# Tanh of the cell state beside the sums in PSUM, a rule for GpSimd's long operations, more buffers for the image's chunks, and new constants for the planner

## The chip, the cores and the metric

The kernel runs on one core of a Trainium2 chip. A core has five engines that run side by side and meet through semaphores: TensorE (PE in the profile, with PEld for its weight loads), VectorE (DVE), ScalarE (ACT), GpSimd (POOL) and SyncE (SP), which here issues all transfers. The metric is the device time of one execution in microseconds; lower is better. Everything is computed in fp32.

## The reference

The input x has 8 images of 56 x 56 positions with 256 channels. Two layers follow each other, cut here to what matters:

```python
# layer 0
x = x + attn0(_gn(x))     # group norm over each image; regional attention: an image is 7 x 7
                          # regions of 8 x 8; each takes the 4 best regions by mean query and key,
                          # and each query the best 32 of these 256 keys (top_k, softmax);
                          # plus a 3 x 3 depthwise convolution of v, then a projection
# layer 1, on the 3136 tokens of each image
t = t + attn1(_ln_t(t))   # attention over 7 neighbouring tokens
t = t + ffn(_ln_t(t))     # a recurrence over the 3136 tokens, for 8 images at once:
def step(carry, xs):
    h, c = carry
    xi_t, xf_t, xg_t, xo_t = xs
    i_t = jax.nn.sigmoid(xi_t + h @ V_i)
    g_t = jnp.tanh(xg_t + h @ V_c)
    o_t = jax.nn.sigmoid(xo_t + h @ V_o)
    c_new = h * c + i_t * g_t
    h_new = o_t * jnp.tanh(c_new)
    return ((h_new, c_new), h_new)
```

## The kernel before

The work comes in two kinds that share all engines. The **attention work** is cut into 56 units: 7 rows of regions (448 tokens each) times 8 images. A unit computes queries and values (`queries_and_lepe`), goes through 7 regions (`region`), projects (`project`), attends over neighbours and makes the recurrence's input terms (`window_attention`). In a region, VectorE does most: four rounds of MAX8 and MATCH_REPLACE8 on 128 x 256 scores for each of four groups of heads find the 32 best keys; GpSimd subtracts what is left from the exponentials (`pe`, 128 x 256). Before an image's first unit, `norm_and_route` reads the image twice in 7 chunks of 448 tokens: `stats(p)` takes sums of a chunk, `keys_values(p)` normalizes a chunk on VectorE, multiplies it by the weights on TensorE, copies keys (`ks`) and values (`vs`) out on ScalarE, and stores them to `kd` and `vd`, from where regions gather them (`kg`, `vg`). A chunk is the tile `xchunk`, with 2 buffers, as have `ks` and `vs`.

The **recurrence** is one chain of 3136 steps (`recurrence`). A step has six instructions that wait for each other: 16 matmuls in one bundle add h times V to a bank of PSUM in which the input terms already stand (`sums`, two banks, two steps to a bank; the terms come by DMA into `r_gin` and are copied in by ScalarE, `place_terms`); VectorE transposes the bank (`r_tr`); ScalarE takes tanh of it into the tile `r_cell`; VectorE's scan makes the new cell state (`r_c`, two inputs, both in SBUF); ScalarE takes its tanh (`r_tc`, in SBUF); VectorE's scalar_tensor_tensor makes h (`r_hs`, from `r_cell` and `r_tc`, both in SBUF). Beside that chain ScalarE makes `r_half`, and GpSimd multiplies it by h into `r_cell` for the next step: this small product is "GpSimd's part of a step". Steps of the first rows run among the attention work of the next row, since a step needs the tokens of all 8 images; the last 451 steps (`step_apart`) run when no other work is left, with the matmuls, the transpose and the first tanh split in two.

The order of all instructions is made when the kernel is built, by a planner written in the kernel (class `_Plan`). Every instruction is recorded with an estimate (`_time`) of how long it holds its engine (`held`) and when its result is there (`late`). `run` then walks through time: whenever an engine is free, it takes the ready instruction of the best rank. Steps of the chain have rank 0, attention work rank 1. An instruction that is not of the chain is taken only if it would end before the next instruction of the chain is expected on that engine, plus `SLACK`; for GpSimd the next "pair" counts, an instruction of VectorE with more than one tensor input (`op.pair`). `at` counts the chain's instructions that have been placed, six to a step. Where TensorE would idle longer than `FILL`, a matmul into a spare bank is put in. The result is one fixed order for each engine's queue; on the chip each queue runs in that order, and instructions wait there only for their data.

Of the kernel before, what the change touches and what calls it, by code (L numbers as in the profile page):

```python
# [10 lines left out]
F32 = mybir.dt.float32  # L11
# [6 lines left out]
SP = mybir.EngineType.SP  # L18

P = 128  # L20
C = 256
NWIN = 7
R = 8
W = NWIN * R
S = R * R
NREG = NWIN * NWIN
ROW = NWIN * S
# [5 lines left out]
QB = 112  # L33
# [11 lines left out]
UJ = C // J  # L45
GJ = GATES * UJ
# [11 lines left out]
HOP = 70  # L58
FAR = 10**12
FILL = 250  # L60
SLACK = {"PE": 120, "DVE": 120, "ACT": 60, "POOL": 60, "SP": 1000}


def _shape_of(shape, pattern, sizes):
# [37 lines left out]
def _time(engine, name, view, reads, args, kw):  # L102

    n = max([_count(v) for v in [view] + reads])
    if engine == "SP":
        return 650, 2600 + n // 2
    if engine == "PE":
        held = 160 if name == "transpose" else 5 * _count(view) // 3 + 110
        return held, held + 200
    if engine == "POOL":  # L110
        t = 180 + 15 * n // 7
        return (1050, 1050) if ALU.pow in args else (t + 90, t)
    if engine == "ACT":
        t = 5 * n // 7 + 100
        if kw.get("accum_out") is not None:
            return t + 150, t + 260
        if isinstance(kw.get("bias"), _View) or view.buf.banks:
            return t + 120, t + 200
        return t + 20, t + 110
    held = 25 * n // 24 + 60  # L120
    if name == "reciprocal":
        return 20 * n // 3 + 60, 20 * n // 3 + 150
    if name == "transpose":
        return held + 40, held + 120
    if name == "tensor_tensor_scan":
        return 2 * n + 80, 2 * n + 170
    if name == "match_replace":
        return held + 65, held + 150
    if name == "scalar_tensor_tensor":
        return held + 20, held + 100  # L130
    return held, held + 90
# [97 lines left out]
class _Plan:  # L229
# [71 lines left out]
    def add(self, engine, traces, reads, writes, held, late):  # L301
        op = _Op()
        op.engine, op.trace, op.held, op.late = engine, traces, held, late
        op.rank, op.chain = self.mode
        op.rank = (op.rank, len(self.ops))
        op.before, op.takes, op.start = {}, [], None
        op.pair = engine == "DVE" and len(reads) > 1
        self.ops.append(op)
        for views, write in ((reads, False), (writes, True)):
            for v in views:  # L310
                self._depend(op, v, write)
                if v.buf.pool is not None:
                    if not v.buf.users:
                        op.takes.append(v.buf)
                    if not v.buf.users or v.buf.users[-1] is not op:
                        v.buf.users.append(op)
# [25 lines left out]
    def run(self, tc, fill):  # L342
# [24 lines left out]
        at, made, events = 0, {}, []  # L367
# [24 lines left out]
                    return t  # L392
            return FAR

        filled = 0
        while len(done) < len(ops) + filled:
            moved = False
            for e in engines:
                if free[e] > now:
                    continue  # L400
                while later[e] and later[e][0][0] <= now:
                    _, rank, op = heappop(later[e])
                    insort(ready[e], (rank, op))
                if not ready[e]:
                    continue
                until = expected(e) + SLACK[e]
                for i, (rank, op) in enumerate(ready[e]):
                    if not op.chain and now + op.held > until:
                        continue
                    if any(b.free and not self._room(b, made, now) for b in op.takes):  # L410
                        continue
                    del ready[e][i]
                    op.start = now
                    free[e] = now + op.held
                    heappush(events, free[e])
                    heappush(events, now + op.late + HOP)
                    done.append(op)
                    for b in op.takes:
                        if b.free:
                            made.setdefault(id(b.tag), []).append(b)  # L420
                    for b, gap in op.before.items():
                        b.due = max(b.due, now + gap)
                        b.open -= 1
                        if not b.open:
                            opened(b)
                    if op.chain:
                        at += 1
                    moved = True
                    break
            if not moved and free["PE"] <= now:  # L430

                due = min([expected("PE")] + [op[0] for op in later["PE"][:1]])
                if FILL < due - now < FAR // 2:
                    op = _Op()
                    op.trace, op.start = [fill], now
                    filled += 1
                    done.append(op)
                    free["PE"] = now + FILL
                    heappush(events, free["PE"])
                    moved = True  # L440
            if not moved:
                while events and events[0] <= now:
                    heappop(events)
                if not events:
                    raise RuntimeError("the plan has stopped")
                now = heappop(events)
# [30 lines left out]
def _layers(ctx: ExitStack, tc, a, out):  # L477
# [9 lines left out]
    nc = tc.nc  # L487
    nb = x.shape[0]
# [7 lines left out]
    two = ctx.enter_context(tc.tile_pool(name="two", bufs=2))  # L496
    small = ctx.enter_context(tc.tile_pool(name="small", bufs=6))
    image = ctx.enter_context(tc.tile_pool(name="image", bufs=1))
    rwork = ctx.enter_context(tc.tile_pool(name="r_work", bufs=3))
# [3 lines left out]
    ps_r = ctx.enter_context(tc.tile_pool(name="ps_r", bufs=1, space=PSUM))  # L503
# [60 lines left out]
    for dy in range(3):  # L564
        rows = slice(dy * HD, (dy + 1) * HD)
        for n in range(24):
            k, dx, g = n // 12, n // 4 % 3, n % 4
# [13 lines left out]
    for t in cells:  # L581

        nc.vector.memset(t, 0.0)
        for at in (0, CELL + 2):
            e = t[:, at : at + CELL].rearrange("p (n e) -> p n e", e=3)
# [2 lines left out]
    gins = [const.tile([P, XB, GJ], F32, name=f"r_gin{i}") for i in range(2)]  # L588
    for t in gins:
        nc.gpsimd.memset(t, 0.0)  # L590
    sums = [ps_r.tile([P, 2 * GJ], F32, name=f"r_sum{i}") for i in range(2)]
    for t in sums:
        nc.tensor.matmul(
            t, gins[0].rearrange("p t g -> p (t g)")[:, :P], wu[:, 0, : t.shape[1]],
            start=True, stop=True, skip_group_check=True,
        )
# [12 lines left out]
    raw, nc = nc, _Plan(nc)  # L609
# [6 lines left out]

    cells = [nc.fixed(t, (P, 3 * CELL + 4)) for t in cells]
    gins = [nc.fixed(t, (P, XB, GJ)) for t in gins]
    sums = [nc.fixed(t, (P, 2 * GJ), banks=1) for t in sums]
    state = {"h": h0}  # L620
    t2, xg = [], []

# [9 lines left out]
    def norm_and_route(b, im):  # L632
# [1 line left out]


        def chunk(p):
            xc = two.tile([P, 2, ROW], F32, name="xchunk")
            nc.sync.dma_start(
                xc, xt[b, :, p * ROW : (p + 1) * ROW].rearrange("(k q) s -> q k s", k=2)
            )  # L640
            return xc
# [67 lines left out]
        def keys_values(p):  # L709
            xn = chunk(p)  # L710
            normalize(im, xn)
            ks = two.tile([P, NWIN, 2, S], F32, name="ks")
            for m in range(2):
                pk = bank()
                for k in range(2):
                    nc.tensor.matmul(
                        pk[:, :ROW], w0[:, k, C + m * P : C + (m + 1) * P],
                        xn[:, k, :], start=(k == 0), stop=(k == 1),
                    )
                nc.scalar.activation(  # L720
                    ks[:, :, m, :], pk[:, :ROW].rearrange("p (q s) -> p q s", s=S),
                    AF.Identity, bias=b0[:, 2 + m : 3 + m],
                )
            nc.sync.dma_start(
                im["kd"][p * NWIN : (p + 1) * NWIN].rearrange("q p s -> p q s"),
                ks.rearrange("p q k s -> p q (k s)"),
            )
            for i in range(NQB):
                pv = bank()
                for k in range(2):  # L730
                    nc.tensor.matmul(
                        pv[:QB, :C], xn[:, k, i * QB : (i + 1) * QB], w0[:, k, 2 * C :],
                        start=(k == 0), stop=(k == 1),
                    )
                vs = two.tile([QB, C], F32, name="vs")
                nc.scalar.copy(vs, pv[:QB, :C])
                t0 = p * ROW + i * QB
                nc.sync.dma_start(im["vd"][t0 : t0 + QB], vs)
# [504 lines left out]
    def place_apart(t, part):  # L1243
        cols = slice(0, 2 * UJ) if part == "ci" else slice(2 * UJ, 3 * UJ)
        nc.scalar.copy(apart(t, part), gins[t // XB % 2][:, t % XB : t % XB + 2, cols])

    def compact(t):
        return t.rearrange("p (c x) -> p c x", x=32)[:, :, :nb]

    def recurrence(blk):  # L1250
# [14 lines left out]
        def step(t):  # L1265
# [7 lines left out]
            with nc.rank(0, chain=True):  # L1273
# [17 lines left out]
                    c.rearrange("p k b e -> p (k b e)"), cell[:, :CELL],  # L1291
                    cell[:, CELL + 2 : 2 * CELL + 2], 0.0, ALU.mult, ALU.add,
                )
                tch = rwork.tile([P, 2, nb], F32, name="r_tc")
                nc.scalar.activation(tch, c[:, :, :, 2], AF.Tanh, scale=0.5)
                hn = hs[:, :, t, :]
                nc.vector.scalar_tensor_tensor(
# [214 lines left out]
```

## Time and profile before

The three runs before took 9910.28, 9912.33 and 9922.73 us (median 9912.33). The profiled execution took 9902.77 us, with a span of 9901.1 us from the first to the last instruction. Its first step of the recurrence ends near 1500 us; the first split step begins at 8890 us.

| stretch of the span, us | length | PE busy | DVE busy | ACT busy | POOL busy |
|---|---|---|---|---|---|
| 0 to 1500: attention of the first row, norms of all images | 1500 | 1239 | 1053 | 678 | 396 |
| 1500 to 9000: attention and steps together | 7500 | 6987 | 6610 | 4801 | 2707 |
| 9000 to 9901: the chain alone | 901 | 778 | 386 | 385 | 91 |

How to read it: busy time is the sum of an engine's instructions in that stretch. Weight loads are counted apart. PE's time holds the spare matmuls too (2208 us in the whole span). In the page's groups a row gives the engine, the operation, the tiles written and read, shape, count, busy time and mean duration, and behind the second bar the engine's idle time before these instructions and what ended it. Line L290 is the planner's one place of recording, so tiles tell the instructions apart.

### The profile page before, as it was taken

What the parts mean: (1) busy time and instruction counts of PE and PEld (TensorE: products, weight loads), DVE (VectorE), ACT (ScalarE), POOL (GpSimd) and SP (SyncE); (2) the same over time, 40 slices, a digit from 0 to 9 for tenths busy, and PEclk for the clock granted to TensorE, in tenths of its full rate; (3) what the DMA queues carried; (4) which work ended last, traced back from release to release, by engine and by line L of the source; (5) the groups of instructions that cost most, each with busy time, mean ns of one, the idle gap of its engine ahead of it and who ended that gap; (6) DMA issues with size and microseconds to landing.
All of it is one profiled execution on the core that took longest, in us unless ns stands there. A gap on an engine that the chain in (4) does not pass through costs nothing.

```text
span 9901.1 us, 320002 instructions
## 1 busy us (share of the span) xinstructions
PE 9004.2 (91%) x111782; PEld 5270.8 (53%) x111782; DVE 8048.2 (81%) x32969; ACT 5863.0 (59%) x22855; POOL 3193.8 (32%) x7550
## 2 busy tenths in 40 slices
PE   6888889999999999999999999999999999998888
PEld 4445445555555555555545555555555545557777
DVE  5686688999998999989989899898988888874444
ACT  3444456666666666666666666666666666654444
POOL 1222233333333333333333333333333333331111
PEclk9989889999999999999999999999999999999999
DMA  5544423233233232332323323233232222220000
GB/s 156 150 131 132 121 82 86 75 80 82 76 82 81 71 83 77 81 81 71 84 74 81 81 72 86 74 81 79 74 85 76 72 73 79 75 53 21 21 21 19
DMA packets 838243, 786.81 MB, mean 79 GB/s; under 512 B 94734, under 2 KB 794244, under 8 KB 836628
## 3 DMA queue, kind: packets, MB, share of 16 engines
q1 hardware_dynamic: 836628, 766.33, 29.1%
q8 instruction: 884, 14.48, 0.6%
q14 instruction: 731, 5.99, 0.2%
HBM read 527.08 MB, written 238.88 MB: 77 GB/s over the span
## 4 chain that ended last, share of the span: by engine, by line
DVE 46%; PE 16%; ACT 12%; DMA 5%; issue 5%; SPq 1%; POOL 1%; DVEq 0%; ACTq 0%; POOLq 0%
DVE left L290 13%; DVE top L290 10%; PE r_sum L290 9%; DVE r_c L290 7%; DVE r_tr L290 7%; ACT r_cell L290 5%; PE mm L290 5%; DVE r_hs L290 4%; DMA vshift<-lines 2%; ACT r_tc L290 2%; DMA lines<-v 2%; PE pt_av L290 1%; DVE st L290 1%; PE spare L604 1%; ACT et L290 1%
## 5 line engine op out<-in xcount | busy, mean ns | idle before, releaser
L290 PE MATMUL r_sum<-r_v,r_hs 128*8 128x192 f32 (+1 forms) x57376 | 2650.4, 307 | 496.1 <-DVE r_hs L290 439.1
L290 POOL TENSOR_TENSOR r_cell<-r_hs,r_half 128x16 f32<-128x16 f32 x3136 | 722.6, 230 | 4643.2 <-DVE r_hs L290 2588.8
L604 PE MATMUL spare<-ident 128*32 128x128 f32 x15904 | 2208.1, 277 | 1.5 <-POOL ident masks.py:199 1.5
L290 ACT ACTIVATE r_cell<-r_tr 128x48 f32<-128x48 f32 (+2 forms) x3587 | 911.7, 259 | 2156.4 <-DVE r_tr L290 2069.5
L290 PEld LDWEIGHTS r_sum<-r_v,r_hs 128*8 128x8 f32 x57376 | 1233.5, 89 | 1739.1 <-DVE r_hs L290 1397.5
L290 DVE MATCH_REPLACE8 left<-top,left 128x256 f32<-128x256 f32 x4704 | 1899.5, 407 | 0.2 <-issue 0.2
L604 PEld LDWEIGHTS spare<-ident 128*32 128x32 f32 x15904 | 1596.3, 110 | 471.9 <-issue 373.2
L290 DVE MAX8 top<-left 128x8 f32<-128x256 f32 x4704 | 1841.1, 406 | 1.4
L290 DVE STREAM_TRANSPOSE r_tr<-r_sum 128x192 f32<-128x192 f32 (+2 forms) x3587 | 1231.9, 350 | 631.1 <-PE r_sum L290 607.0
L290 DVE TENSOR_TENSOR_SCAN r_c<-r_cell 128x48 f32<-128x48 f32 x3136 | 945.5, 302 | 542.3 <-ACT r_cell L290 382.3
L290 POOL TENSOR_TENSOR pe<-pe,left 128x256 f32<-128x256 f32 x1568 | 1142.1, 733 | 731.2 <-ACT left L290 590.7
L290 ACT ACTIVATE r_tc<-r_c 128x16 f32<-128x16 f32 x3136 | 701.1, 224 | 508.9 <-DVE r_c L290 469.9
L290 ACT COPY r_sum<-r_gin 128x384 f32<-128x384 f32 (+2 forms) x1795 | 807.7, 450 | 14.1 <-DMA r_gin<-xgd 7.8
L290 ACT ACTIVATE pe<-sc,nmax 128x256 f32<-128x256 f32 x1568 | 684.9, 472 | 173.0 <-DVE left L290 103.4
L290 PE MATMUL pt_av<-ident,pe 128*128 128x128 f32 x3136 | 690.5, 297 | 91.2 <-POOL pe L290 67.2
L290 ACT ACTIVATE left<-left,nmax 128x256 f32<-128x256 f32 x1568 | 749.1, 500 | 35.5 <-DVE left L290 26.3
L290 DVE SCALAR_TENSOR_TENSOR r_hs<-r_cell,r_tc 128x16 f32<-128x16 f32 x3136 | 587.9, 187 | 188.8 <-ACT r_tc L290 183.7
L290 PE MATMUL mm<-wu,xlT 128*112 128x512 f32 (+2 forms) x1856 | 728.1, 509 | 3.2 <-ACT gs L290 2.5
L290 ACT ACTIVATE et<-top,nmax 128x32 f32<-128x32 f32 x1568 | 497.3, 318 | 332.8 <-DVE top L290 325.4
L290 DVE MAX8 top<-sc 128x8 f32<-128x256 f32 x1568 | 618.2, 412 | 78.6 <-PE sc L290 75.2
L290 ACT COPY pts<-pt_av 128x256 f32<-128x256 f32 x1568 | 566.0, 361 | 169.5 <-PE pt_av L290 166.8
L290 ACT ACTIVATE r_half<-r_c 128x16 f32<-128x16 f32 x3136 | 651.4, 208 | 0.0
(128 smaller groups left out, 11793.0 us busy)
## 6 DMA issues: line engine op xcount, KB each, us to landing
kg<-kd SPq DMA_DIRECT2D x1568, 64.0 KB
vg<-vd SPq DMA_DIRECT2D x1568, 64.0 KB
vshift<-lines SPq DMA_DIRECT2D x336, 232.0 KB
xgd<-gs SPq DMA_DIRECT2D x224, 336.0 KB
r_gin<-xgd SPq DMA_DIRECT2D x1568, 48.0 KB
xchunk<-xt SPq DMA_DIRECT2D x112, 448.0 KB
lines<-v SPq DMA_DIRECT2D x112, 290.0 KB
xn<-xh SPq DMA_DIRECT2D x56, 560.0 KB
```

Of the source, the lines that this page charges most:

```text
L290: method(*[v.real() if isinstance(v, _View) else v for v in args], **{k: v.real() if isinstance(v, _View) else v for k, v in kw.items()},)
L604: raw.tensor.matmul(spare[:32, :P], ident[:, :32], ident, start=True, stop=True, skip_group_check=True)
```

## The change

In the step, the tanh of the cell state is written to 16 more columns of the PSUM bank that holds the step's sums, and the instruction that makes h reads it there:

```diff
-    sums = [ps_r.tile([P, 2 * GJ], F32, name=f"r_sum{i}") for i in range(2)]
+    sums = [ps_r.tile([P, 2 * GJ + 2 * nb], F32, name=f"r_sum{i}") for i in range(2)]
...
+    def cell_tanh(t):
+
+        bank = sums[t // 2 % 2]
+        return bank[:, 2 * GJ :].rearrange("p (k b) -> p k b", k=2)
...
-                tch = rwork.tile([P, 2, nb], F32, name="r_tc")
+                tch = cell_tanh(at)
                 nc.scalar.activation(tch, c[:, :, :, 2], AF.Tanh, scale=0.5)
```

This is in `step` alone; `step_apart` is not edited and keeps its tile `r_tc`. In the planner, instructions of GpSimd that hold it for more than 400 ns get a condition, a "pair" is now one with two inputs in SBUF, and some constants change:

```diff
-SLACK = {"PE": 120, "DVE": 120, "ACT": 60, "POOL": 60, "SP": 1000}
+LONG = 400
+SLACK = {"PE": 60, "DVE": 120, "ACT": 60, "POOL": 60, "SP": 1000}
...
     if engine == "SP":
-        return 650, 2600 + n // 2
+        return 650, 2400 + 9 * n // 4
...
-        if isinstance(kw.get("bias"), _View) or view.buf.banks:
+        if isinstance(kw.get("bias"), _View) or view.buf.banks and n > UJ:
...
-        op.pair = engine == "DVE" and len(reads) > 1
+        op.pair = engine == "DVE" and sum(not v.buf.banks for v in reads) > 1
...
-        filled = 0
+        filled = tied = 0
...
+                    if e == "POOL" and op.held > LONG and (at % 6 > 3 or tied < at // 6):
+
+                        continue
...
                     if op.chain:
                         at += 1
+                    elif e == "POOL" and op.rank[0] == 0:
+                        tied += 1
```

The chunk's tile `xchunk` gets 4 buffers instead of 2, `ks` 3, `vs` 4. No computation is added or removed; both programs have 26691 instructions of VectorE and 21057 of ScalarE.

More of the change, by code (lines that the diff above doesn't have):

```diff
@@ L590, in _layers @@
         nc.gpsimd.memset(t, 0.0)
-    sums = [ps_r.tile([P, 2 * GJ], F32, name=f"r_sum{i}") for i in range(2)]
+    sums = [ps_r.tile([P, 2 * GJ + 2 * nb], F32, name=f"r_sum{i}") for i in range(2)]
     for t in sums:
+        t = t[:, : 2 * GJ]
         nc.tensor.matmul(
@@ L618, in _layers @@
     gins = [nc.fixed(t, (P, XB, GJ)) for t in gins]
-    sums = [nc.fixed(t, (P, 2 * GJ), banks=1) for t in sums]
+    sums = [nc.fixed(t, (P, 2 * GJ + 2 * nb), banks=1) for t in sums]
     state = {"h": h0}
@@ L636, in chunk @@
         def chunk(p):
-            xc = two.tile([P, 2, ROW], F32, name="xchunk")
+            xc = two.tile([P, 2, ROW], F32, name="xchunk", bufs=4)
             nc.sync.dma_start(
@@ L711, in keys_values @@
             normalize(im, xn)
-            ks = two.tile([P, NWIN, 2, S], F32, name="ks")
+            ks = two.tile([P, NWIN, 2, S], F32, name="ks", bufs=3)
             for m in range(2):
@@ L734, in keys_values @@
                     )
-                vs = two.tile([QB, C], F32, name="vs")
+                vs = two.tile([QB, C], F32, name="vs", bufs=4)
                 nc.scalar.copy(vs, pv[:QB, :C])
```

## The prediction

> **What bounds the kernel now.** I read the slices of the page first, then the timeline of some steps in the middle, the groups by form, the waits of the first 1500 us, and the timeline of one stretch there.
>
> ```profile
> span 9901.1 us, 320002 instructions
> DVE  5686688999998999989989899898988888874444
> ACT  3444456666666666666666666666666666654444
> ```
>
> VectorE is busy for about 90% from slice 7 to slice 36, less before (norms) and after (the chain alone). From the first step (1500.2 us) to the first split step (8890.1) lie 2685 steps, 2.75 us each. Averaged over them, the chain's path is: end of r_hs to the transpose 1088 ns, transpose 373, to the gates' tanh 101, that tanh 268, to the scan 105, scan 309, to the cell's tanh 36, that tanh 224, to r_hs 55, r_hs 190. The shortest times that recur for these pieces add up to about 2512 ns, so some 236 ns a step are lost to other work. Two causes stand in the timeline:
>
> ```profile
> 5003.66 0.73 POOL L290 TENSOR_TENSOR pe<-pe,left 128x256 f32<-128x256 f32 x1 [1.24 <-ACT left L290]
> 5003.85 0.64 DVE L290 TENSOR_TENSOR_SCAN r_c<-r_cell 128x48 f32<-128x48 f32 x1 [0.15 <-ACT r_cell L290]
> ...
> 5009.49 0.26 DVE L290 TENSOR_TENSOR_SCAN r_c<-r_cell 128x48 f32<-128x48 f32 x1
> 5009.78 0.22 ACT L290 ACTIVATE r_tc<-r_c 128x16 f32<-128x16 f32 x1
> ...
> 5011.24 0.37 DVE L290 STREAM_TRANSPOSE r_tr<-r_sum 128x192 f32<-128x192 f32 x1
> 5011.71 0.27 ACT L290 ACTIVATE r_cell<-r_tr 128x48 f32<-128x48 f32 x1 [1.59 <-DVE r_tr L290]
> ```
>
> A scan that meets a long GpSimd operation takes 0.64 us, one that doesn't 0.26. And the cell's tanh starts 0.03 us behind the scan, the gates' tanh 0.10 behind the transpose: in the program the first waits for one semaphore, the second for two. Over the trace these gaps are 34 and 94 ns (the same tile with one wait: 34), so a second wait costs 60 ns where the late one comes first.
>
> **The change, part by part.** Every term is set against the span of 9901.1.
>
> ```profile
> L290 DVE TENSOR_TENSOR_SCAN r_c<-r_cell 128x48 f32<-128x48 f32 x3136 | 945.5, 302 | 542.3 <-ACT r_cell L290 382.3 <-POOL gs L290 20.8 <-POOL pe L290 5.4
> L290 DVE SCALAR_TENSOR_TENSOR r_hs<-r_cell,r_tc 128x16 f32<-128x16 f32 x3136 | 587.9, 187 | 188.8 <-ACT r_tc L290 183.7
> L290 DVE SCALAR_TENSOR_TENSOR r_res<-mm,r_res 128x128 f32<-128x128 f32 x392 | 102.8, 270 | 2.1 <-PE mm L290 1.6 <-issue 0.5
> L290 DVE SCALAR_TENSOR_TENSOR s<-mm,mask 112x118 f32<-112x118 f32 x224 | 58.8, 263 | 15.2 <-PE mm L290 15.1
> L290 ACT COPY r_sum<-r_gin 128x256 f32<-128x256 f32 x226 | 82.1, 363 | 1.8 <-DMA r_gin<-xgd 1.8
> L290 ACT COPY r_sum<-r_gin 128x128 f32<-128x128 f32 x226 | 61.8, 274 | 0.8 <-DMA xgd<-gs 0.3 <-ACT r_cell L290 0.3
> ```
>
> *r_hs meets GpSimd no more: -52.* Its median is 174 ns; 191 of 3136 are longer by more than 20, together 52 us, nearly all under a long GpSimd operation (median there 443). Forms with one input in PSUM, r_res and s, have the same median under a long GpSimd operation (270, 262) as without (267, 261). With r_tc in PSUM, r_hs becomes such a form. Bounds -52 and 0.
>
> *The scan still meets it: +16.* The scan keeps two inputs in SBUF. 536 scans are lengthened, by 138 us in all; by the programs' order 508 of them (132 us) by a long operation that stands on GpSimd's queue just ahead of GpSimd's part of the coming step: its data are there early, so it starts about 1.3 us before the h that the planner put it behind. The new condition should forbid that place, but `tied` counts every rank-0 instruction of GpSimd, also the memset of `r_hs` in the first block, and so runs one ahead. In the order of the changed program 1299 long operations still stand there, against 1167; none is left between scan and r_hs (35 before). 138 x 1299/1167 = 154. Bounds -138 (collisions gone) and +60 (every added one hits).
>
> *The cell's tanh: +20.* Of the 2685 steps, 1605 get a second wait: the tanh now writes a bank that TensorE writes, so the sequencer waits for VectorE (late) and the instruction for TensorE (long done). Behind it on ScalarE stands r_half, which feeds GpSimd's part; that part ends a median 1.47 us before the next scan, so only r_hs is late. The write itself: copies into PSUM take 274 ns at 128 elements, 363 at 256, 495 at 384; the lines through them give 159 to 196 at 16, against 208 for r_half's copy into SBUF: 12 to 49 less, I take 30. From scan to r_hs VectorE has other work too. Where it is nothing or one short instruction (56% of the steps) the wait ends at 290 ns by the tanh; with one MATCH_REPLACE8 (28%) VectorE itself ends at 295; with two (15%) later. So a step with the second wait loses 0.56 x 30 + 0.28 x 25 = 24 ns, one without gains 0.56 x 30 = 17: 1605 x 24 - 1080 x 17 = +20 us. With no gain from PSUM +79, with 49 about -15. The split steps keep r_tc and don't change.
>
> *r_hs reads PSUM: -14.* r_res, s and part (277 at 128), carried to 16 elements at 1.04 ns an element, give 153 to 160 against 174: 17 less, which reaches the chain where TensorE and not VectorE ends the wait for the transpose, about 30% of the steps: 17 x 0.3 x 2685. The dearest such row, t (476 at 256, with a pointer scalar too), gives 226: +52 a step, 140 us if all of it counts. Most rows lie near 157, so I take that.
>
> By the Trainium skill (Perfetto Trace Analysis, Optimizing Scalar/DVE Operations) ScalarE's overhead is 93 ns on SBUF and 51 on PSUM, VectorE's 60 and 125. That speaks against this edit: tanh 42 shorter, r_hs 65 longer. The trace's VectorE rows don't bear it out; the second rival below is that case.
>
> *Estimates and SLACK: -35.* TensorE starts r_sum late by 152 us in all; 46 of this behind convolutions that wait for `vshift` at the head of its queue. The planner now expects that transfer 3 us later (2400 + 9n/4 for 2600 + n/2, n = 1856), and its upper quartile of steps between issue and use goes from 2 to 3: I take 25. Of 54 us behind ordinary attention matmuls, the smaller SLACK takes 10. Bounds 0 and -100. VectorE's order in a step hardly moves: 8.2 instructions a step, as before, and the attention work ends by step 2685 in both.
>
> *Buffers: -80.* In the first 1500 us:
>
> ```profile
> DVE xchunk L290 <- DMA xchunk<-xt: 164.8, 33, 12.8
> ...
> ACT vs L290 <- DMA vd<-vs: 81.2, 51, 4.1
> ```
> ```profile
> 474.91 0.40 SPq L290 DMA_DIRECT2D xchunk<-xt  x1
> 475.75 0.67 ACT L290 COPY vs<-mm 112x256 f32<-112x256 f32 x2 [2.14 <-DMA vd<-vs]
> ...
> 478.82 0.94 DVE L290 TENSOR_SCALAR xchunk<-xchunk,gm,grs 128x448 f32<-128x448 f32 x2 [9.40 <-DMA xchunk<-xt]
> ```
>
> While chunks of keys and values are made, VectorE stands still: the next chunk is issued late, because a buffer must come free and the stores of `vs` stand before it on SP's queue; ScalarE waits for stores that still read `vs`. The 48 intervals between chunks of one image average 10.3 us; TensorE needs 3.3 + 3.7 = 7.0 a chunk. So at most 48 x 3.3 = 157 us are to be had. The new order has 2 to 3 chunks in flight for the first four of most images; I take half. It could be +20, if early loads hold up gathers behind them on SP.
>
> **Sum:** -52 + 16 + 20 - 14 - 35 - 80 = -145: a span of 9756. The median of the runs lies 11 us above this span (9912.33), so 9767.
>
> **Rivals.**
> *The first stage gains nothing.* For: TensorE is busy 1239 of the 1500 us already, and its clock is granted at about 0.9 there. Against: the waits above. 9767 + 80 = 9847.
> *PSUM costs more than it saves: slower.* Place: from scan to r_hs. The second wait at its full price with no faster write (+79), r_hs 52 ns longer on all steps (+140): -52 + 16 + 79 + 140 - 35 - 80 = +68, so 9980. It decides from 54 ns a step (145/2685) above my forecast. For: the row t, and that the wait is certain. Against: r_res, s, part. The skill's rule named above is of this kind.
> *The condition works as named:* if the order that I read misleads, scans are freed: 9767 - 154 = 9613. Against: 1299 operations in the wrong place.
> *Nothing to see:* full second waits and no gain in the first stage: -52 + 16 + 79 - 14 - 35 = -6, 9906.
>
> **Chances.** Forecast 0.56, first stage unchanged 0.18, PSUM dearer 0.17, condition works 0.04, nothing 0.05. Two tenths of a per cent (20 us) is about what can be told from no change. Faster 0.78 (0.56 + 0.18 + 0.04), same 0.05, slower 0.17. The forecast's own range is 9650 to 9870 by the bounds of the buffers and the estimates; toward the slower case I reach to 9915 and downward to 9640, which leaves out most of the dear PSUM and the working condition.
>
> **What would show it.** Right: r_hs with no long ones and a median near 157; the scan's mean still near 305; the gap from scan to tanh 94 ns in some 60% of the steps; less VectorE time waiting for xchunk, the first step before 1450 us; the split steps unchanged at 2.23 us. Wrong: r_hs above 200 ns, the first step still at 1500, or scans near 260 throughout.

## The result and the profile after

The changed kernel takes 9681.54 us (median of four runs, 9671.93 to 9690.36), the kernel before, run in the same session, 9917.53 (9910.28 to 9936.62). The ratio is 0.9759, with a 95% interval of 0.9741 to 0.9777: 236 us faster, where 145 were forecast. The page's head, with the busy tenths of VectorE and ScalarE over the 40 slices:

```profile
span 9670.2 us, 320850 instructions
...
DVE  6687789898889999989989989899898888864444
ACT  3454556666666666666666666666666666654444
```

VectorE is busier in the first seven slices (6687789 for 5686688). The span is 231 us shorter, and this comes from two places: the first h starts at 1400.5 us (before 1500.2), and the 2685 steps up to the first split one take 7261.0 us (before 7391.1). The split steps cost what they did, 2.23 us each.

The groups by form of the changed kernel that answer to those shown of before (line, engine, operation, tiles, shape, count; busy time and mean ns; then the idle time before them and what ended it):

```profile
L291 DVE TENSOR_TENSOR_SCAN r_c<-r_cell 128x48 f32<-128x48 f32 x3136 | 927.6, 296 | 533.0 <-ACT r_cell L291 381.0 <-POOL pe L291 9.5 <-POOL gs L291 8.6
L291 ACT ACTIVATE r_sum<-r_c 128x16 f32<-128x16 f32 x2685 | 523.2, 195 | 735.9 <-DVE r_c L291 632.7 <-PE pt_av L291 22.7 <-PE mm L291 22.5
L291 DVE SCALAR_TENSOR_TENSOR r_hs<-r_cell,r_sum 128x16 f32<-128x16 f32 x2685 | 455.7, 170 | 80.0 <-ACT r_sum L291 72.9
...
L291 ACT ACTIVATE r_tc<-r_c 128x16 f32<-128x16 f32 x451 | 100.5, 223 | 69.1 <-DVE r_c L291 56.3
```

The cell's tanh is 28 ns shorter where it writes PSUM (195) than in the split steps that keep the tile in SBUF (223). r_hs has a mean of 170 for 187, but the tile's own view (count: shortest/median/longest ns, first and last start), of before and then of after, says where that comes from:

```profile
L290 DVE SCALAR_TENSOR_TENSOR r_hs<-r_cell,r_tc x3136: 138/174/802, 1500.2 to 9896.5; 128x16 f32<-128x16 f32 x196
```
```profile
L291 DVE SCALAR_TENSOR_TENSOR r_hs<-r_cell,r_sum x2685: 138/174/182, 1400.5 to 8649.8; 128x16 f32<-128x16 f32 x192
```

The median is 174 in both. Reading PSUM saves nothing; what is gone is the long tail (longest 182 for 802), the meetings with GpSimd. The scan has kept its meetings: 452 are lengthened, by 120 us in all (before 536, 138 us). The timeline shows one (start, duration in us):

```profile
5054.43 0.72 POOL L291 TENSOR_TENSOR pe<-pe,left 128x256 f32<-128x256 f32 x1 [1.31 <-ACT left L291]
5054.61 0.66 DVE L291 TENSOR_TENSOR_SCAN r_c<-r_cell 128x48 f32<-128x48 f32 x1 [0.48 <-ACT r_cell L291]
```

The second wait of the cell's tanh is there too, some steps earlier in the same timeline:

```profile
5008.00 0.31 DVE L291 TENSOR_TENSOR_SCAN r_c<-r_cell 128x48 f32<-128x48 f32 x1
5008.41 0.19 ACT L291 ACTIVATE r_sum<-r_c 128x16 f32<-128x16 f32 x1
```

The scan ends at 5008.31 and the tanh starts 0.10 us later, where before it took 0.03. Over the trace, the gap lies within 6 ns of 94 in 1572 of the 1601 steps whose tanh waits for more than one semaphore, and within 6 ns of 34 in 1055 of the 1084 where it waits for one. In the first 1500 us the waits (engine, tile, what it waited for: us in total, times, longest) fell by half for `xchunk` and vanished for the stores of `vs`; ScalarE now waits for TensorE there:

```profile
ACT vs L291 <- PE mm L291: 83.4, 169, 1.3
DVE xchunk L291 <- DMA xchunk<-xt: 83.3, 17, 11.1
```

### The profile page after: what moved, and what is told of

It reads as the page before. It is cut to its first block, busy times and chain, and to the rows that moved or that the text cites. A ratio compares the mean times of both kernels' runs of the same rounds, so it can differ in the third digit from the quotient of the medians.

```text
span 9670.2 us, 320850 instructions
## 1 busy us (share of the span) xinstructions
PE 8920.8 (92%) x111412; PEld 5210.1 (54%) x111412; DVE 7978.3 (83%) x32969; ACT 5941.6 (61%) x22855; POOL 3187.1 (33%) x7550
## 5 line engine op out<-in xcount | busy, mean ns | idle before, releaser
L611 PEld LDWEIGHTS spare<-ident 128*32 128x32 f32 x15534 | 1551.0, 110 | 502.5 <-issue 396.6
L291 ACT ACTIVATE r_sum<-r_c 128x16 f32<-128x16 f32 x2685 | 523.2, 195 | 735.9 <-DVE r_c L291 632.7
L291 ACT ACTIVATE pe<-sc,nmax 128x256 f32<-128x256 f32 x1568 | 705.5, 470 | 121.9 <-DVE left L291 76.0
L291 PE MATMUL mm<-wu,xlT 128*112 128x256 f32 (+2 forms) x1856 | 724.8, 510 | 7.0 <-ACT xlT L291 6.6
L291 PEld LDWEIGHTS pt_av<-ident,pe 128*128 128x128 f32 x3136 | 357.8, 144 | 552.5 <-issue 274.8
```

What stands on the lines that cost most here:

```text
L291: method(*[v.real() if isinstance(v, _View) else v for v in args], **{k: v.real() if isinstance(v, _View) else v for k, v in kw.items()},)
L611: raw.tensor.matmul(spare[:32, :P], ident[:, :32], ident, start=True, stop=True, skip_group_check=True)
```

## The experiments

Twelve kernels were run, each against the kernel before. "First step" is where the first h starts; "steps" the time from there to the h of the first split step; "row ends" what six steps, each waiting for the last unit of a row, take beyond a median step; "TensorE late" the sum over the steps of what lies between r_hs and the first weight load of `r_sum` beyond 60 ns (the waits at the first five row ends are in it too, so the two columns must not be added); the last two columns are what scans and r_hs take beyond their medians (only those over 20 ns). All in us, from the profiled executions; the ratios are of the timed runs. "Plan" is the length that the planner itself gives the order that it lays down, in its own estimated times (`self.length` in the kernel, in us), and the brackets have what the six row ends take in that plan.

| kernel | us | ratio (95%) | plan | first step | steps | row ends (planned) | TensorE late | scans | r_hs |
|---|---|---|---|---|---|---|---|---|---|
| before | 9917.5 | 1 | 9489 | 1500 | 7391 | 63 (58) | 152 | 138 | 52 |
| changed | 9681.5 | 0.9759 (0.9741 to 0.9777) | 9474 | 1401 | 7261 | 61 (63) | 78 | 120 | 0 |
| e1_buffers | 9857.0 | 0.9944 (0.9927 to 0.9961) | 9459 | 1451 | 7390 | 64 (58) | 150 | 140 | 49 |
| e2_estimate | 9745.0 | 0.9827 (0.9810 to 0.9843) | 9476 | 1455 | 7284 | 22 (24) | 41 | 112 | 72 |
| e10_both | 9694.7 | 0.9771 (0.9755 to 0.9787) | 9452 | 1407 | 7272 | 22 (24) | 39 | 113 | 71 |
| e7_old_estimate | 9975.4 | 1.0048 (1.0032 to 1.0063) | 9571 | 1448 | 7519 | 195 (187) | 283 | 117 | 0 |
| e3_psum | 9932.7 | 1.0013 (1.0004 to 1.0023) | 9536 | 1496 | 7426 | 104 (98) | 213 | 118 | 0 |
| e6_sbuf | 9621.1 | 0.9696 (0.9680 to 0.9712) | 9416 | 1404 | 7209 | 22 (23) | 44 | 121 | 59 |
| e12_rule_alone | 9618.6 | 0.9701 (0.9685 to 0.9717) | 9416 | 1403 | 7202 | 22 (23) | 44 | 121 | 57 |
| e5_other_bank | 9638.8 | 0.9714 (0.9698 to 0.9730) | 9522 | 1410 | 7218 | 114 (113) | 159 | 149 | 0 |
| e11_no_rule | 9745.5 | 0.9822 (0.9805 to 0.9838) | 9420 | 1401 | 7323 | 27 (27) | 41 | 240 | 38 |
| e4_named | 9829.5 | 0.9917 (0.9900 to 0.9933) | 9675 | 1407 | 7404 | 277 (280) | 283 | 3 | 0 |
| e8_old_slack | 9682.4 | 0.9758 (0.9742 to 0.9774) | 9462 | 1408 | 7265 | 15 (18) | 44 | 129 | 0 |
| e9_null | 9680.7 | 0.9754 (0.9737 to 0.9770) | 9474 | 1411 | 7266 | 61 (63) | 79 | 119 | 0 |

### Buffers and estimate, each alone and together

The kernel before with the buffers alone (e1_buffers):

```diff
-            xc = two.tile([P, 2, ROW], F32, name="xchunk")
+            xc = two.tile([P, 2, ROW], F32, name="xchunk", bufs=4)
...
-            ks = two.tile([P, NWIN, 2, S], F32, name="ks")
+            ks = two.tile([P, NWIN, 2, S], F32, name="ks", bufs=3)
...
-                vs = two.tile([QB, C], F32, name="vs")
+                vs = two.tile([QB, C], F32, name="vs", bufs=4)
```

> The kernel before with the buffers alone (xchunk 4, ks 3, vs 4). Theory: the 100 us of the first stage come from the buffers. Then the first step's r_hs starts between 1395 and 1425 us (before 1500, after 1400), the steps stay at 2.75 us, and the ratio to before is 0.990 to 0.992. Rival: they come from the planner's longer estimates of transfers, which put the loads earlier in SP's order; then the first step stays at 1480 or later and the ratio is 0.998 to 1.000.

Measured: 0.9944, so about 56 us (1 - 0.9944, times 9917.5), short of the 80 to 100 us of the theory and clear of its rival. The first step comes 50 us earlier and the steps are as before, in every column of the table. The buffers act in the first stage and nowhere else.

The kernel before with the new estimate of a transfer's time alone (e2_estimate):

```diff
-        return 650, 2600 + n // 2
+        return 650, 2400 + 9 * n // 4
```

> The kernel before with SP's estimate alone (2400 + 9n/4). Theory: TensorE's late starts of r_sum (152 us in all before, 78 after) fall by 40 to 75 us, the late starts behind vshift nearly vanish, and the first stage moves by less than 25 us: ratio 0.992 to 0.996. Rival: the late starts fell because of the smaller SLACK of TensorE or because the whole order was shuffled; then they stay above 130 us and the ratio is 0.998 to 1.002.

Measured: 0.9827, some 172 us, far beyond both expectations: one entry of the planner is worth three times the buffers, 45 us of it ahead of the first step and 107 on the steps. The trace of before shows one thing that it removes. TensorE and the lines around it, in the timeline:

```profile
4438.70 0.44 DVE L290 SCALAR_TENSOR_TENSOR r_hs<-r_cell,r_tc 128x16 f32<-128x16 f32 x1
...
4440.93 1.72 PE L290 MATMUL mm<-vshift,diag 96*32 96x448 f32 x8 [3.41 <-DMA vshift<-lines]
4442.58 0.29 PEld L290 LDWEIGHTS pt_av<-ident,pe 128*128 128x128 f32 x2 [1.45 <-issue]
...
4443.21 0.10 PEld L290 LDWEIGHTS r_sum<-r_v,r_hs 128*8 128x8 f32 x4
```

h is there at 4439.14 us. But a convolution stands ahead of the step's matmuls on TensorE's queue and waits 3.41 us for its `vshift`; the step's first weights are loaded at 4443.21, 4.07 us late. The same wait in the waits from 1500 to 8880 us, of before, of e2_estimate and of e7_old_estimate; the rows of GpSimd are for the transfer just ahead, `lines`, from which `vshift` is read:

```profile
POOL v L290 <- DMA lines<-v: 105.3, 43, 5.8
PE mm L290 <- DMA vshift<-lines: 78.2, 50, 4.1
```
```profile
POOL v L290 <- DMA lines<-v: 77.2, 36, 5.6
```
```profile
POOL v L291 <- DMA lines<-v: 81.8, 39, 8.0
PE mm L291 <- DMA vshift<-lines: 67.3, 42, 4.8
```

In e2_estimate TensorE has no row for `vshift` any more. With the longer estimate the planner leaves a median of 7.7 us between a `vshift` transfer's issue and the next use of such a tile; before it left 5.4. Away from the row ends, TensorE's late starts fall from 101 us to 38.

Such a wait can cost more than its own length, for the granted clock may drop behind it. A stretch with the wait above and the one that follows (length, busy us and count of PE, PEld, DVE, ACT and POOL, granted clock, share and GB/s of DMA):

```profile
4440.00:4447.00 7.00, 6.07 (x38) 2.17 (x38) 2.24 (x10) 1.35 (x5) 0.24 (x3) 0.51 0.74 201
4447.00:4457.00 10.00, 8.73 (x154) 4.81 (x156) 7.87 (x33) 6.16 (x23) 2.98 (x8) 1.00 0.21 57
```

Between 1500 and 8890 us before has 14 such stretches of half the clock, 68 us in all, every one behind a convolution that waited for `vshift`; the steps around them take 62 us beyond a median step, waits included. In e2_estimate there is one stretch of 3.4 us, in the changed kernel one of 6.8.

The row ends are another matter. At each of the first five, before spends 12.6 to 13.0 us on one step, and e2_estimate 2.9, 2.9, 2.9, 2.9 and 5.6. These waits don't come from transfers that land later than planned: the planner's own order already has them, 9.2 us beyond a median step at each of the five and 12.3 at the last, and with the new estimate next to nothing at four. So it is in all fourteen rows of the table: the row ends measured lie within 9 us of those planned. Row ends give 41 of the 107 us. What other steps of over 3.6 us take beyond a median one (87 us to 12) would more than fill the rest; r_hs, lengthened by 72 us for 52, takes 20 of it back.

Ahead of the first step the plan got 18 us longer (first h at 1408 us for 1390) and the measured time 45 shorter, so here, too, the gain is in waits that the old plan didn't have. The granted clock doesn't explain it: its mean over the first 1400 us is 0.90 before, 0.91 here and 0.89 with the buffers alone. The estimate holds for every transfer, so this run doesn't tell how much of the gain is that of `vshift` and how much that of others.

Both together on the kernel before (e10_both, the two diffs above):

> The kernel before with the new buffers and the new estimate of SP's transfers, nothing else: tanh in SBUF, pairs, SLACK and the rule for GpSimd as before. Theory 1 (the two add up, since one acts in the first stage and the other mostly on the steps): 9917 - 60 - 172 = 9685 us, first step near 1405, the steps near 7285, so that all other parts of the change together are worth nothing. Theory 2 (the rest of the change, rule and r_hs out of GpSimd's way, brings the 36 us or more of steps that it seems to): the same 9685 for this kernel but only if the two overlap is it above 9720; then the rest brings the difference to 9682.

Measured: 0.9771, some 227 us, beside 56 + 172 = 228 for the two alone. They add up, and they are as much as the whole change (0.9759; the intervals overlap). So all that the change does to the recurrence's step and to GpSimd is worth nothing that can be told, as a sum. The reverse, the changed kernel with the old estimate (e7_old_estimate: the diff of e2_estimate turned round):

> The changed kernel with SP's old estimate (2600 + n/2). Theory: TensorE's late starts of r_sum come back (78 us to 130-150), the time rises by 40 to 75 us: ratio 0.980 to 0.984. Rival: they don't, since TensorE's SLACK does it: ratio 0.975 to 0.978.

Measured: 1.0048, slower than before and beyond both expectations. Late transfers hurt no more than they did: away from the row ends TensorE is late by 105 us, as before (101). What is new is row ends of 195 us, and 187 of them stand in the plan. With the old estimate the rest of the change gets a worse order.

### The cell's tanh: PSUM or SBUF

The kernel before with the tanh in PSUM and nothing else but the planner's time for it (e3_psum): the diff of `sums` and `cell_tanh` of the change, and

```diff
-        if isinstance(kw.get("bias"), _View) or view.buf.banks:
+        if isinstance(kw.get("bias"), _View) or view.buf.banks and n > UJ:
```

> The kernel before with the tanh in PSUM alone (columns of the bank and the planner's time for such a write; pairs as before). Theory: no r_hs is lengthened (-52 us), the tanh takes 195 ns, 1630 of 2685 steps have a second wait and lose some of it again (+29 us as after): ratio 0.997 to 0.998. Rival: the second wait eats it all; ratio 1.000 or more. Rival: the wait is hidden behind VectorE's other work; ratio 0.994 or less.

Measured: 1.0013 (1.0004 to 1.0023). No r_hs is lengthened any more, which frees 52 us, and still the steps take 35 us longer: from scan to r_hs a step takes 328 ns for 315 (72 + 195 + 61 for 36 + 224 + 55), and the row ends take 104 us for 63, 98 for 58 in the plan.

The reverse: the changed kernel with the tanh back in its tile, at first in such a way that the planner still doesn't take r_hs for a pair (e6_sbuf):

```diff
-        op.pair = engine == "DVE" and sum(not v.buf.banks for v in reads) > 1
+        op.pair = engine == "DVE" and sum(not v.buf.banks and v.buf.name != "r_tc" for v in reads) > 1
...
-                tch = cell_tanh(at)
+                tch = rwork.tile([P, 2, nb], F32, name="r_tc")
```

> The changed kernel with the tanh back in SBUF; the planner still takes r_hs as no pair. Theory: r_hs is lengthened again by 50 us or more in all (GpSimd's operations may now lie under it), the second waits go (gap 34 ns), the tanh takes 223 ns: together +10 to +40 us, ratio 0.977 to 0.980. Rival: the PSUM tile brings much more, by the order that follows from it: +60 or more, ratio above 0.982. Rival: it brings nothing: 0.974 to 0.976.

Measured: 0.9696, 60 us faster than the changed kernel, where every theory had it as slow or slower. The edit that the change is named after costs. The trade can be read in the pieces of a step, means over 2685 steps in ns, here against e12_rule_alone, which differs from the changed kernel by the tile alone, and by the order that the planner makes of it:

| | r_hs to transpose | scan to tanh | tanh | tanh to r_hs | r_hs |
|---|---|---|---|---|---|
| e12_rule_alone (SBUF) | 1031 | 36 | 224 | 48 | 192 |
| changed (PSUM) | 1055 | 72 | 195 | 59 | 170 |

PSUM takes 29 from the tanh and 22 from r_hs; it adds 36 by the second wait and 11 ahead of r_hs. These four make -4. What decides is the first column, 24 more behind r_hs: 11 of them at the first five row ends and 13 in the other steps, where the transpose starts 128 ns behind the last matmul for 118. The loss stands in the order before anything runs: the plan of the changed kernel is 58 us longer (9474 for 9416), some 40 of it at row ends. The row ends alone aren't the price of the tile, since e8_old_slack, below, has short ones (15 us) and takes the changed kernel's time. What in the planning makes the order longer was not isolated.

The changed kernel with the tanh in the other bank, the one that TensorE isn't about to write (e5_other_bank):

```diff
-        bank = sums[t // 2 % 2]
+        bank = sums[1 - t // 2 % 2]
```

> The changed kernel with the tanh in the other of the two banks, whose last matmul lies a step or more back: 145 steps instead of 1605 have a second wait. Theory: the second wait costs what the stretch from scan to r_hs lost; the gap from scan to tanh goes from 72 to about 38 ns on average, the stretch from 326 to 285-300 ns, and the time falls by 60 to 90 us against the changed kernel: ratio 0.967 to 0.970. Rival: VectorE's own work between scan and r_hs, or the order of the rest, takes up most of it: 10 to 30 us, ratio 0.973 to 0.976.

Measured: 0.9714, 43 us faster than the changed kernel. The tanh has its second wait in 145 steps instead of 1605, and scan to tanh has a mean of 40 ns for 72. The gates' tanh starts 72 ns behind the transpose for 100, which nobody had expected: there, too, the second wait fell out of half the steps (1365 of 2685 wait for one semaphore; in the changed kernel 34). Some of it is lost again at the row ends (114 us), and it stays behind the SBUF tile. The plan knows nothing of this gain: it is 48 us longer than the changed kernel's.

### The rule for GpSimd's long operations

The changed kernel whose `tied` doesn't count the memset, so that the rule does what its words say (e4_named):

```diff
-                    elif e == "POOL" and op.rank[0] == 0:
+                    elif e == "POOL" and op.rank[0] == 0 and not op.takes:
```

> The changed kernel with the condition as it is named: tied counts GpSimd's part of a step alone, not the memset in the first block. No long operation stands between r_hs and GpSimd's part in the order any more (1299 after). Theory: the scans' 120 us go away, scans' mean 258 to 265 ns, and the time is some 115 us below the changed kernel's: ratio 0.962 to 0.968. Rival: with the window from GpSimd's part to the scan (about 1.5 us) only one long operation of 0.73 us fits a step, there is one a step on average, so the subtractions come late, the attention work waits and steps get longer or rows end with gaps: ratio 0.976 or above, even with short scans.

Measured: 0.9917, 148 us slower than the changed kernel, although the scans are freed as in no other version:

```profile
L291 DVE TENSOR_TENSOR_SCAN r_c<-r_cell 128x48 f32<-128x48 f32 x3136 | 811.1, 259 | 559.3 <-ACT r_cell L291 419.2 <-POOL r_cell L291 8.4 <-ACT pts L291 1.8
```

The mean is 259 ns, 3 us are lost in all, and a usual step (the mean without the six row ends) takes 2.655 us for 2.682. But GpSimd's long operations now have only one place in a step, the attention work falls behind, and the chain waits for it where a row ends. The r_hs of e4_named and of e12_rule_alone between 2580 and 2637 us, where the steps of the first 448 tokens end:

```profile
L291 DVE SCALAR_TENSOR_TENSOR r_hs<-r_cell,r_sum x5: 164/174/175, 2580.2 to 2634.8; 128x16 f32<-128x16 f32 x5
```
```profile
L291 DVE SCALAR_TENSOR_TENSOR r_hs<-r_cell,r_tc x16: 158/174/451, 2580.8 to 2636.7; 128x16 f32<-128x16 f32 x16
```

Five steps for sixteen: one step took 47 us. So it is at five row ends (46 to 47 us each) and at the last (59), 277 us in sum, and 280 in the plan. Being one ahead is what lets the changed kernel's rule be bearable.

The changed kernel with the tanh in SBUF, r_hs no pair, and the rule switched off (e11_no_rule: e6_sbuf with `LONG = 400000`):

> The changed kernel with the cell's tanh in its SBUF tile (as in the run that took 9621) and the rule for GpSimd's long operations switched off (LONG 400000 ns). Theory 1 (the rule, though one ahead, brings the 60 us by which that run beats the kernel before with buffers and estimate): 9670 to 9700 us. Theory 2 (the rule does next to nothing, since 121 us of lengthened scans stayed; the gain over buffers and estimate comes from r_hs being no pair for the planner, or from the order): 9600 to 9640 us, scans lengthened by 110 to 140 us as before.

Measured: 0.9822, 124 us slower than e6_sbuf with the rule. That is slower than the first theory had it, and it refutes the second. The scan of e11_no_rule:

```profile
L291 DVE TENSOR_TENSOR_SCAN r_c<-r_cell 128x48 f32<-128x48 f32 x3136 | 1048.9, 334 | 492.4 <-ACT r_cell L291 341.5 <-POOL pe L291 11.5 <-POOL gs L291 8.3
```

Its mean is 334 ns, and 240 us are lost. The order shows why: once r_hs is no pair, the planner puts some 1200 long operations between scan and r_hs, but GpSimd has their data early and starts them before that scan, and over 550 hit it. The plan doesn't see such a meeting: it is only 4 us longer than that of e6_sbuf. The rule forbids just that place. What remains to ask is what it does where r_hs is a pair, as with the tile in SBUF and the change's own definition (e12_rule_alone: the changed kernel with only the last line of e6_sbuf's diff):

> The changed kernel with the cell's tanh back in its SBUF tile, and r_hs therefore again a pair for the planner (in the run that took 9621 it was none): buffers, estimate, SLACK and the rule for GpSimd's long operations. The kernel before with buffers and estimate took 9695; without the rule and with r_hs as no pair 9745; with the rule and r_hs as no pair 9621. Theory 1 (the rule works on its own: it keeps long operations from between the scan and r_hs and spreads them, whatever the pairs are): 9605 to 9640 us, so the rule is worth some 70 us over buffers and estimate, and the tanh in PSUM can go altogether. Theory 2 (the rule only repairs what the new pairs open; with the old pairs the planner keeps GpSimd back twice, behind the rule and ahead of r_hs, and the attention work falls behind as in the kernel whose condition worked as named): 9690 to 9800 us, with waits at the row ends above 100 us in sum instead of 22.

Measured: 0.9701, the same as e6_sbuf (0.9696) and 70 us faster than e10_both (0.9771), with intervals that don't touch. So the rule, with the new SLACK, is worth some 70 us on top of buffers and estimate, and this is the fastest version: 63 us less than the changed kernel. The scans explain none of it (121 us lost for 113), nor do the row ends (22 and 22). By the pieces of a step, 9 ns came off between r_hs and the transpose, 7 ahead of r_hs (48 for 56) and 6 off r_hs (192 for 198), which is 59 of the 70 us on 2685 steps. Of the 70, 37 stand in the plan (9452 to 9416). What in the order of VectorE's queue does it was not isolated, nor rule and SLACK apart in this kernel.

### Two controls

SLACK of TensorE back to 120 in the changed kernel (e8_old_slack), and VectorE's at 121 for 120 (e9_null), which nothing has a price for:

```diff
-SLACK = {"PE": 60, "DVE": 120, "ACT": 60, "POOL": 60, "SP": 1000}
+SLACK = {"PE": 120, "DVE": 120, "ACT": 60, "POOL": 60, "SP": 1000}
```
```diff
-SLACK = {"PE": 60, "DVE": 120, "ACT": 60, "POOL": 60, "SP": 1000}
+SLACK = {"PE": 60, "DVE": 121, "ACT": 60, "POOL": 60, "SP": 1000}
```

> The changed kernel with TensorE's old SLACK (120). Theory: late starts behind ordinary attention matmuls rise by about 10 us, ratio 0.976 to 0.978. Rival: SLACK is what took 74 us off TensorE's late starts; then they are above 120 us again and the ratio is 0.982 or more.

> The changed kernel with one constant moved by one part in 120: VectorE's SLACK 121 ns for 120. It changes nothing that any theory has a price for, but the planner's choices differ from some point on, so the order is another of the same kind. Theory 1 (the differences of 40 us and more between the variants come from what was edited): 9660 to 9705 us, beside 9682 for the changed kernel. Theory 2 (a new order is worth some tens of us by itself, whatever was edited): more than 30 us away from 9682, on either side; then the 60 us for the tanh's place and the 43 us for the bank are within what an order gives by chance.

Measured: 0.9758 and 0.9754, both the changed kernel's 0.9759. The smaller SLACK is worth nothing: it shortens a usual step (2.682 us for 2.700) and pays with row ends (61 us for 15). The null moves instructions (VectorE's order has another one at 731 of 26597 places, by tile names), and the time stays, so the 43 to 148 us between the other variants are not what any small reshuffling gives. It is one control, and its order is closer to the changed kernel's than those of the large edits are: its plan is as long (9474) and has the same row ends.

## Why the prediction was right or wrong

The side and the range were right, the size was not: 236 us for 145. That the sum stayed inside the range is partly luck: estimates and rule brought 223 us more than forecast, the tanh's place and the buffers 128 less. Step by step:

- **What bounds the kernel.** Right. The gain lies in the first stage and in what a step loses to other work; the split steps didn't change.
- **r_hs meets GpSimd no more, -52.** The mechanism was right and the trace shows it: none lengthened. As time it didn't arrive by itself: e3_psum frees the same 52 us and is slower, in an order with longer row ends.
- **The scan still meets it, +16.** The reading of `tied` was right: 452 scans are still lengthened, some 440 of them by operations just ahead of GpSimd's part. The size was off (120 us, not 154). What was missed is that the rule pays in another way: some 70 us with the tile in SBUF (together with the new SLACK).
- **The cell's tanh, +20.** Close. The second wait is 60 ns, the tanh 28 shorter, and scan to r_hs takes 326 ns for 315: 11 x 2685 = 29 us. The rows for the write left more room than the working says: the line through the two longer copies, carried to 16 elements, gives about 115 ns, not 159.
- **r_hs reads PSUM, -14.** Wrong. The median stayed at 174: the rows r_res, s and part, carried to 16 elements, didn't tell r_hs's time.
- **Estimates and SLACK, -35, bounds 0 and -100.** This step failed most. The estimate alone brings 172 us, the SLACK nothing. The forecast counted TensorE's late starts behind a convolution (46 us, 25 taken). Away from the row ends these late starts fell by 63 us in all, and with them went the stretches of half the clock that followed such waits. It put two more things at nothing: the row ends, where the planner's own order waited 58 us and with the new estimate 24 (measured 63 and 22), and the 45 us in the first stage, where the estimate also holds for the chunks' transfers. That the chunks' transfers are the cause there is argued: e2_estimate shows the 45 us, not which transfer.
- **Buffers, -80.** Right in place; 56 us alone.

The measured steps add up in the order in which they were told apart: -56 (buffers), -172 (estimate), -70 (rule), +58 (0.9759 - 0.9701, the tanh's place) make -240, for -239 by the ratio. So the term of the two edits of the tanh (-52 + 20 - 14 = -46) had the wrong sign.

Of the rivals, "PSUM costs more than it saves" was right in its sign and wrong in its price and place: r_hs isn't longer, the second wait is about paid for by the faster tanh and by r_hs without its long tail, and the loss lies in the order behind r_hs. By the Trainium skill (Perfetto Trace Analysis, Optimizing Scalar/DVE Operations) ScalarE's overhead is 42 ns less on PSUM (~51 for ~93) and VectorE's 65 more (~125 for ~60). The trace has 28 less for the tanh and no difference for r_hs. "The condition works as named" gave 9613: e4_named does what that rival described, frees 117 us of scans and takes 9829.5, since the rival forgot who would be late: work that is moved off the chain has to be done by the row's end, and the plan of that kernel waits 280 us there.

## What to carry to other kernels

Where a planner lays down a fixed order, set its own times beside the measured ones. What already stands in the plan, here the waits at the row ends and the 58 us of the tile, can be read without a run. What does not is what the estimates leave out: waits for transfers, meetings with GpSimd, second waits. Look at the estimates of transfers first: one that is too short puts a consumer at the head of a queue, and here that cost the wait, the slower clock behind it, and an order with longer row ends. A plan alone is no forecast: it has e5_other_bank 48 us slower than the changed kernel, and that one was 43 us faster. Before keeping work away from a place on an engine, count who waits for that work and where the deadline is; a place that is free of collisions for the chain may be the only time that the other work had. And test the parts of a change apart: here one estimate and three buffer counts carried the result, and the part that the title names first cost 58 us.

## What the runs showed of the hardware

- A VectorE instruction with two inputs in SBUF that starts under a long GpSimd operation and is held ends at a fixed time behind it, however long it was held: the scan 114 ns after the GpSimd operation's end (quartiles 113 and 114, 452 scans of the changed kernel), r_hs 29 ns after (28 and 30, 191 of before). In the timeline above, 5054.43 + 0.72 = 5055.15 and 5054.61 + 0.66 = 5055.27. The Trainium skill (SBUF — State Buffer, SBUF: two separate sides) calls the port that the two share an exclusive lock, held for the whole instruction. The trace agrees for VectorE held by GpSimd, and r_hs with one input in PSUM (longest 182 ns) falls out of the lock.
- A second semaphore wait costs 60 ns where the late one comes first (34 and 94 ns from scan to tanh, in 1055 and 1572 steps of the changed kernel). In this kernel the bank that is written decides whether it is there: 1605 steps with the one, 145 with the other.
- Behind a TensorE that stood idle the granted clock was seen to drop to half, for 3.4 to 10.2 us: in the steps of before, behind each of the six waits for `vshift` of more than 3 us (3.0 to 4.1) and behind eight of the shorter ones. With the waits gone the stretches are gone (14 before, one in e2_estimate).
- ScalarE's copies of 128 x 384 into the bank took 480 ns where the bank holds the tanh's columns too, and 495 where it doesn't. Why was not looked into.
